# A decoder layer on one core: two self-attention units and one cross-attention unit to a period

## The chip, the core and the metric

The kernel runs on one core of a Trainium2 chip. Its engines work side by side, each through its own queue of instructions: TensorE (PE in the profile, its weight loads PEld) multiplies matrices into the accumulation memory PSUM, VectorE (DVE) and ScalarE (ACT) read PSUM and work element by element, GpSimd (POOL) does element work on SBUF, and SyncE (SP) issues most transfers. Semaphores order the engines among each other. The metric is the time of one execution on the device, in microseconds (us). Three runs of the kernel before took 2284.96, 2285.08 and 2286.03 us; the median is 2285.08.

## The reference

One layer of a decoder for 32 sequences of 256 tokens, width 256, all in float32 but for the feed-forward's quantised products. Cut to what matters:

```python
# self attention: 16 heads of 64, 4 key/value heads, rotary positions, ALiBi, no causal mask
attn = einsum('bhqd,bhkd->bhqk', rope(x @ Wq), rope(x @ Wk)) / sqrt(64) + slopes * (k - q)
x = layernorm(x + merge(softmax(attn) @ v) @ Wo)
# cross attention to ctx: 16 heads of 16, each projection behind its own layer norm,
# windows of 64 (own and preceding), causal, and only between tokens of equal cell number
p = where(mask, rope(qh) @ rope(kh).T / sqrt(16), lowest)
x = layernorm(x + ln(merge(softmax(p) @ vh)) @ w_o.T + b_o)
# feed-forward 256 -> 1024 -> 256: activations rounded to 8 bits, weights to -1, 0, 1
x = layernorm(x + bitlinear(silu(bitlinear(x, w_gate)) * bitlinear(x, w_up), w_down))
```

## The kernel before, in words

A sequence (called a batch, `b`) is worked on in stages, and several batches are under way at a time. Nothing is carried between batches but buffers.

**Self attention.** A batch has eight self units: (128 queries `qc`, key/value pair `kc`, head pair group `rp`), four heads each. `self_scores` multiplies `qT` by `kT` on PE with 64 rows (one head in each half of the array), into two PSUM banks `s`; DVE adds the ALiBi row, negates, and finds the minimum (`p`, `nm`, L410); ACT exponentiates in place and sums (L420). `self_turn` transposes the four heads' `p` on PE (`t`, L447), and ACT copies the result to `pT` (L452). Two units make a pair, and for a pair `self_values` multiplies `v` by `pT` (`o`, L464, 64 columns a head), ACT copies to `oT`; `self_inverse` (DVE) and `self_spread` (PE, `R`, L479) bring the reciprocal sums into shape, and `self_normal` multiplies `oT` by them on DVE. `self_output` multiplies by `Wo` (`wo`, L495), adds the residual, and makes the query of cross attention: stats on DVE, `rs` on POOL (L510 to L513), the normed row `zq` on DVE, its transposition `zqT`, the projection `xq`, `biased` (`qb` on ACT, partition exchange `other` by DMA) and `rotated` (three POOL products).

**Cross attention.** A batch has four cross units (128 queries, half of the heads). `cross_scores` runs 32-row tiles into four banks `xs` (L656); DVE masks and finds the minimum (`xp`, `xnm`, L670); `cross_exp` on ACT (L686), in two halves; `cross_turn` (PE `xt`, L695, ACT `xpT`, L697); `cross_values` with 32-column tiles (`xo`, L711), ACT copies to `xoT`; `cross_back` transposes back (`xr`, L731) and divides on DVE. `cross_output` norms, transposes (`zoT`, ACT copy `zT`), multiplies by the output weights (`xw`, L757) and adds the residual.

**Feed-forward.** `feed_forward` multiplies by gate and up weights in bf16 (`ff`), with tanh on ACT (L812) and products on DVE (L813, L819), quantises through POOL (`tr`, L785; `gu`, L834), transposes by DMA and multiplies by the down weights (`ffo`, L845). `self_inputs` and `cross_inputs` load and project a batch (`proj`, L331; `v`; `zcT`; `xk`; `xv`), two batches' lead ahead.

**The order.** PE, DVE and ACT get their instructions in the order in which the code is run; POOL and SP are ordered by the framework. The order is written by hand in a loop over slots: two slots are a step, a step takes one self unit, and a cross unit begins at every other step. Longer stages are generators; each `yield n` puts the rest n slots later, and they are started at slots counted from `s0 = 16 * b`. `last` holds ACT work that `flush` puts at the end of a slot. All PSUM tiles come from one pool of eight banks. In the even slot of a step:

```python
own(self_turn, step - 1)
if odd:
    cross(cross_back, k - 1)
    cross(cross_turn, k, 0)
else:
    cross(cross_turn, k - 1, 1)
flush()
own(self_scores, step)
if not odd:
    cross(cross_scores, k)
pair(self_values)
```

So, of two steps, one has s, xs and, in its second slot, the projections of other stages and xo; the other has s, o and R.

Of the kernel before, what the change touches and what calls it, by code (L numbers as in the profile page):

```python
# [9 lines left out]
F32 = mybir.dt.float32  # L10
BF16 = mybir.dt.bfloat16
# [5 lines left out]
P = 128  # L17
# [33 lines left out]
def kernel(  # L51
# [33 lines left out]
    def ctile(shape, dtype, name):  # L85
        return const.tile(shape, dtype, name=name, tag=name)
# [6 lines left out]

    ident = ctile([P, P], F32, "ident")
    make_identity(nc, ident)
    ident_b = ctile([P, P], BF16, "ident_b")
    make_identity(nc, ident_b)
    neg_half = ctile([P, 2], F32, "neg_half")
    nc.gpsimd.memset(neg_half, -0.5)

# [285 lines left out]
    def self_scores(b, i):  # L386
        s = state[b]
        qc, kc, rp = self_units[i]
        qT, kT = s["qT", 2 * kc + rp], s["kT"]
        banks = [bank("s") for _ in range(2)]  # L390
        for rr in range(2):
            for half in range(2):
                rows_ = slice(half * HD, (half + 1) * HD)
                nc.tensor.matmul(  # L394
                    banks[half][:, rr * L : (rr + 1) * L],
                    qT[rows_, rr, qc * P : (qc + 1) * P],
                    kT[rows_, kc, :],
                    start=(rr == 0),
                    stop=(rr == 1),
                )  # L400
        s["p", i] = [work("p", [P, 512], 4) for _ in range(2)]
        if rp == 0:
            s["sums", i // 2] = small("sums", 8)
        for half in range(2):
            p = s["p", i][half]
            nm = small("nm", 2)
            for rr in range(2):
                cols = slice(rr * L, (rr + 1) * L)

                nc.vector.tensor_tensor_reduce(  # L410
                    p[:, cols],
                    banks[half][:, cols],
                    alibi[:, 2 * (4 * kc + 2 * rp + rr) + half, :],
                    -0.125,
                    3.0e38,
                    ALU.add,
                    ALU.min,
                    nm[:, rr : rr + 1],
                )
                nc.scalar.activation(  # L420
                    p[:, cols],
                    p[:, cols],
                    AF.Exp,
                    bias=nm[:, rr : rr + 1],
                    scale=-1.0,
                    accum_out=s["sums", i // 2][:, (2 * rp + rr) * 2 + half : (2 * rp + rr) * 2 + half + 1],
                )

    def self_inverse(b, m):

# [58 lines left out]
    def self_output(b, qc):  # L489

        s = state[b]
        py = bank("wo")
        for kc in range(2):
            for r in range(NCH // 2):
                nc.tensor.matmul(  # L495
                    py[:, 0:D],
                    s["oT", qc, kc][:, r, :],
                    wo_sb[:, 4 * kc + r, :],
                    start=(kc == 0 and r == 0),
                    stop=(kc == 1 and r == 3),  # L500
                )
            if kc == 0:
                yield
        h = work("row", [P, D], 6)
        nc.vector.tensor_tensor(h, py[:, 0:D], s["xs"][:, qc, :], ALU.add)
        mv = stats(h, "x1")


        rs = small("rs_x1", 3)
        nc.gpsimd.tensor_scalar(rs[:, 0:1], mv[:, 1:2], EPS, None, ALU.add)  # L510
        nc.gpsimd.tensor_scalar(rs[:, 1:2], mv[:, 1:2], 1.0 + EPS, EPS * EPS, ALU.mult, ALU.add)
        nc.gpsimd.tensor_tensor(rs[:, 0:2], rs[:, 0:2], neg_half, ALU.pow)
        nc.gpsimd.tensor_scalar(rs[:, 2:3], mv[:, 0:1], rs[:, 0:1], -1.0, ALU.mult, ALU.mult)  # L513
        yield
        zq = work("row", [P, D], 6)
        nc.vector.tensor_scalar(zq, h, mv[:, 0:1], rs[:, 1:2], ALU.subtract, ALU.mult)

        s["x1", qc] = x1 = work("x1", [P, D], 4)

        def residual():  # L520
            nc.scalar.activation(x1, h, AF.Identity, bias=rs[:, 2:3], scale=rs[:, 0:1])
            nc.gpsimd.tensor_tensor(x1, x1, xbias[O_], ALU.add)

        last.append(residual)
        yield
        zqT = work("zT", [P, NDC, P])
        transposed(zqT, zq, "zqT")
        yield 2
        pq = bank("xq")
        for ch in range(NDC):  # L530
            for dc in range(NDC):
                nc.tensor.matmul(
                    pq[:, ch * P : (ch + 1) * P],
                    xq_w[:, dc, ch * P : (ch + 1) * P],
                    zqT[:, dc, :],
                    start=(dc == 0),
                    stop=(dc == NDC - 1),
                )
        s["xqT", qc] = work("xqT", [P, NDC, P])
        pair = biased(pq, Q_, P)  # L540
        yield 2
        rotated(s["xqT", qc], *pair, 0, qc * P)


# [25 lines left out]
    def cross_inputs(b):  # L570
# [10 lines left out]
        zc = cs  # L581
        for t in range(NT):
            last.append(partial(scaled, zc[:, t, :], cs[:, t, :], rstds[t]))
        ck = work("ck", [P, L], 1)
        nc.gpsimd.tensor_copy(ck, ck_i)
        yield 2
        zcT = work("tr", [P, NDC, L], 3)
# [156 lines left out]
    def cross_output(b, t):  # L744
        s = state[b]
        on = s["on", t]
        mv = stats(on, "zo")
        rstd = rstd_of(mv, "zo")
        yield
        last.append(partial(scaled, on, on, rstd))  # L750
        yield
        zoT = work("zT", [P, NDC, P])
        transposed(zoT, on, "zoT")
        yield
        py = bank("xw")
        for dc in range(NDC):
            nc.tensor.matmul(py[:, 0:D], zoT[:, dc, :], xo_w[:, dc, :], start=(dc == 0), stop=(dc == NDC - 1))  # L757
        if t == 0:
            s["x2"] = work("x2", [P, NT, D])
        h = s["x2"][:, t, :]  # L760
        nc.vector.tensor_tensor(h, py[:, 0:D], s["x1", t], ALU.add)
        mv = stats(h, "x2")
        rstd = rstd_of(mv, "x2")
        yield
        last.append(partial(scaled, h, h, rstd))


    def feed_forward(b):
# [53 lines left out]
        for t in range(NT):  # L822
# [10 lines left out]
            d_ofs.append(d_of)  # L833
            nc.gpsimd.tensor_scalar(gu[:, t, :], gu[:, t, :], hup, MAGIC, ALU.mult, ALU.add)  # L834
            yield
            hib = work("hib", [P, INNER], 1, BF16)
            nc.vector.tensor_scalar(hib, gu[:, t, :], MAGIC, None, ALU.subtract)
            hiT = work("hiT", [P, NIC, P], 2, BF16)
            nc.sync.dma_start_transpose(hiT, hib)
# [17 lines left out]

    CROSS = 9  # L860
    state = {b: {} for b in range(B)}
    starts = {}

# [7 lines left out]
    for b in range(B):  # L871
        s0 = 16 * b
        if b:
            at(s0 - 16, self_inputs(b))
        at(s0 + 2, cross_inputs(b))
        for t in range(NT):
            at(s0 + 2 * (5 + 4 * t), self_output(b, t))
            at(s0 + 2 * (CROSS + 5 + 4 * t) + 1, cross_output(b, t))
        at(s0 + 2 * (CROSS + 11) + 2, feed_forward(b))

    with tc.manual_schedule(engines={mybir.EngineType.PE, mybir.EngineType.DVE, mybir.EngineType.Activation}):
        running = []
        slot = min(starts)
        while starts or running:
            step, part = divmod(slot, 2)
            k, odd = divmod(step - CROSS, 2)
            for gen in starts.pop(slot, ()):
                running.append([slot, gen])

            def cross(f, unit, *more):  # L890
                if 0 <= unit < 4 * B:
                    f(*divmod(unit, 4), *more)

            def own(f, unit):
                if 0 <= unit < 8 * B:
                    f(*divmod(unit, 8))


            def pair(f):
                if step % 2 == 0 and 0 <= step // 2 - 1 < 4 * B:  # L900
                    f(*divmod(step // 2 - 1, 4))

            if part == 0:
                pair(self_inverse)
            else:
                pair(self_spread)
            if part == 1 and not odd:
                cross(cross_exp, k, 0)
            if part == 0 and odd:
                cross(cross_exp, k, 1)  # L910
            for r in list(running):
                if r[0] == slot:
                    wait = next(r[1], r)
                    if wait is r:
                        running.remove(r)
                    else:
                        r[0] += wait or 1
            if part == 0:
                own(self_turn, step - 1)
                if odd:  # L920
                    cross(cross_back, k - 1)
                    cross(cross_turn, k, 0)
                else:
                    cross(cross_turn, k - 1, 1)
                flush()
                own(self_scores, step)
                if not odd:
                    cross(cross_scores, k)
                pair(self_values)
            else:  # L930
                if not odd:
                    cross(cross_values, k - 1)
                pair(self_normal)
            flush()
            slot += 1

# [88 lines left out]
```

## Time and profile before

The profiled execution took 2288.16 us on the device; its span, from the first to the last instruction, is 2286.3 us. Granted TensorE clock: 0.985 of full over the span.

| engine | busy us | share of the span |
|---|---|---|
| PE | 2186.2 | 96% |
| PEld | 1653.7 | 72% |
| DVE | 1709.6 | 75% |
| ACT | 1692.1 | 74% |
| POOL | 1117.3 | 49% |

A page of the profile shows busy time of each engine, the chain of work that ended last, and groups of equal instructions by line with what ended the idle time before them. The timeline gives instructions in order of time, equal neighbours merged: start, length, engine, line, operation, tiles written and read, and how many. For PE, lengths overlap (a matmul begins before its predecessor's modelled end), so one start is compared with the next. A fp32 product stands there as two instructions. Costliest groups on the engines beside PE: the exponentials (L420) 507.9 us of ACT in 1024 instructions, and the passes over the scores (L410) 372.3 us of DVE in 1024.

### The profile page before, as it was taken

The numbers are of one execution on the slowest core, as the hardware profiler recorded it, in microseconds if no ns is written. First come the engines' busy times: TensorE is split into PE (matmuls) and PEld (weight loads), VectorE is DVE, ScalarE is ACT, GpSimd is POOL, SyncE is SP. The second block draws the span as 40 slices with busy tenths as digits, with TensorE's granted clock in tenths as the row PEclk, the third lists the DMA queues.
The fourth block names the chain that finished last, engine by engine and source line by source line (L and its number), as shares of the span: only waits on it lengthen the run. The fifth ranks groups of instructions, "written<-read, shape, count | busy, mean of one in ns | idle before, by whom it ended". The sixth has DMA issues, their size and how long they took to land.

```text
span 2286.3 us, 55642 instructions
## 1 busy us (share of the span) xinstructions
PE 2186.2 (96%) x17828; PEld 1653.7 (72%) x17828; DVE 1709.6 (75%) x6949; ACT 1692.1 (74%) x4961; POOL 1117.3 (49%) x1851
## 2 busy tenths in 40 slices
PE   7999999999999999999999999999999999999983
PEld 5677777777777777777777777777777777777651
DVE  3767777877777777777777777787777787777675
ACT  2677777878777878777878777778777777777762
POOL 5344555554555444545554545454545454545432
PEclk9999999999999999999999999999999999999986
DMA  6312222222222222222222222222222222222111
GB/s 215 89 52 55 65 67 59 58 58 59 66 66 59 59 58 63 64 64 60 60 58 67 57 64 63 60 57 68 55 65 62 62 54 68 59 57 56 31 31 31
DMA packets 191427, 144.09 MB, mean 63 GB/s; under 512 B 107808, under 2 KB 160928, under 8 KB 191136
## 3 DMA queue, kind: packets, MB, share of 16 engines
q1 hardware_dynamic: 189440, 136.95, 24.3%
q8 instruction: 144, 2.36, 0.4%
q10 hardware_dynamic: 1696, 3.57, 0.4%
q14 instruction: 147, 1.20, 0.2%
HBM read 39.50 MB, written 8.39 MB: 21 GB/s over the span
## 4 chain that ended last, share of the span: by engine, by line
PE 71%; DVE 12%; ACT 11%; DMA 2%; issue 2%; POOL 1%; SPq 0%; ACTq 0%; POOLq 0%; DVEq 0%
PE s L394 10%; PE proj L331 10%; PE wo L495 9%; PE t L447 8%; PE o L464 8%; ACT p L420 4%; DVE p L410 4%; PE xt L695 4%; DVE gu L813 3%; PE xw L757 3%; ACT xp L686 3%; PE xv L616 3%; PE ffo L845 2%; PE R L479 2%; PE xk L604 2%; PE v L363 2%
## 5 line engine op out<-in xcount | busy, mean ns | idle before, releaser
L420 ACT ACTIVATE p<-p,nm 128x256 f32<-128x256 f32 x1024 | 507.9, 498 | 156.1 <-DVE nm L410 152.3
L410 DVE CUSTOM_DVE_ANT_0 p<-s,alibi 128x256 f32<-128x256 f32 x1024 | 372.3, 420 | 167.8 <-PE s L394 167.8
L452 ACT COPY pT<-t 128x512 f32<-128x512 f32 x512 | 274.8, 590 | 190.7 <-PE t L447 190.1
L686 ACT ACTIVATE xp<-xp,xnm 128x128 f32<-128x128 f32 x1024 | 326.0, 394 | 4.3 <-DVE xnm L670 4.3
L394 PE MATMUL s<-kT,qT 64*128 64x256 f32 x2048 | 290.9, 403 | 0.0
L447 PE MATMUL t<-ident,p 128*128 128x128 f32 x2048 | 269.2, 274 | 3.2 <-ACT p L420 3.2
L447 PEld LDWEIGHTS t<-ident,p 128*128 128x128 f32 x2048 | 240.4, 141 | 34.8 <-ACT p L420 6.6
L464 PE MATMUL o<-pT,v 128*64 128x256 f32 x2048 | 249.3, 385 | 0.0
L331 PE MATMUL proj<-xT,wq_sb 128*128 128x256 f32 x1024 | 249.1, 387 | 0.0
L495 PE MATMUL wo<-wo_sb,oT 128*128 128x256 f32 x1024 | 245.3, 382 | 0.0
L355 POOL TENSOR_TENSOR qT<-qT,other 128x512 f32<-128x512 f32 x128 | 163.7, 1279 | 152.0 <-DMA other<-psin 83.7
L670 DVE CUSTOM_DVE_ANT_0 xp<-xs,mask 128x128 f32<-128x128 f32 x1024 | 225.7, 286 | 0.9 <-PE xs L656 0.9
L394 PEld LDWEIGHTS s<-kT,qT 64*128 64x128 f32 x2048 | 176.6, 186 | 54.7 <-issue 32.8
L495 PEld LDWEIGHTS wo<-wo_sb,oT 128*128 128x128 f32 x1024 | 189.4, 190 | 33.8 <-issue 10.6
L331 PEld LDWEIGHTS proj<-xT,wq_sb 128*128 128x128 f32 x1024 | 185.6, 191 | 32.7 <-DVE xnm L670 5.9
L464 PEld LDWEIGHTS o<-pT,v 128*64 128x64 f32 x2048 | 136.0, 136 | 97.4 <-issue 41.1
L420 ACT ACTIVATION_READ_ACCUMULATOR p<-p,nm 128x1 f32 x1024 | 192.4, 188 | 0.0
L340 DVE TENSOR_TENSOR psin<-proj,rs_sb 128x512 f32<-128x512 f32 x160 | 110.2, 689 | 96.7 <-PE proj L331 96.5
L697 ACT COPY xpT<-xt 128x512 f32<-128x512 f32 x256 | 153.6, 600 | 8.3 <-PE xt L695 6.6
L695 PE MATMUL xt<-ident,xp 128*128 128x128 f32 x1024 | 155.1, 275 | 0.0
L566 POOL TENSOR_TENSOR qb<-qb,rx_sb 128x256 f32<-128x256 f32 (+1 forms) x96 | 87.7, 913 | 128.9 <-ACT xp L686 76.6
L813 DVE SCALAR_TENSOR_TENSOR gu<-gu,ff 128x512 f32<-128x512 f32 x128 | 82.1, 681 | 74.6 <-ACT gu L812 74.6
(150 smaller groups left out, 4365.0 us busy)
## 6 DMA issues: line engine op xcount, KB each, us to landing
other<-psin SPq DMA_DIRECT2D x640, 64.0 KB, 2.0
xT<-in_xt_dram SPq DMA_DIRECT2D x32, 256.0 KB, 2.9
xs<-in_x_dram SPq DMA_DIRECT2D x32, 256.0 KB, 3.1
cs<-in_ctx_dram SPq DMA_DIRECT2D x32, 256.0 KB, 2.7
other<-qb SPq DMA_DIRECT2D x64, 128.0 KB, 2.0
kTz<-tr SPq DMA_DIRECT2D x256, 32.0 KB, 2.0
other<-qb SPq DMA_DIRECT2D x128, 64.0 KB, 1.9
out_dram<-x SPq DMA_DIRECT2D x32, 256.0 KB, 2.3
```

What stands on the lines that cost most here:

```text
L331: nc.tensor.matmul(pq[:, c * L : (c + 1) * L], w[:, dc, c * P : (c + 1) * P], xT[:, dc, :], start=(dc == 0), stop=(dc == NDC - 1),)
L355: nc.gpsimd.tensor_tensor(d2, d2, other, ALU.add)
L394: nc.tensor.matmul(banks[half][:, rr * L : (rr + 1) * L], qT[rows_, rr, qc * P : (qc + 1) * P], kT[rows_, kc, :], start=(rr == 0), stop=(r ...
L410: nc.vector.tensor_tensor_reduce(p[:, cols], banks[half][:, cols], alibi[:, 2 * (4 * kc + 2 * rp + rr) + half, :], -0.125, 3.0e38, ALU.add ...
L420: nc.scalar.activation(p[:, cols], p[:, cols], AF.Exp, bias=nm[:, rr : rr + 1], scale=-1.0, accum_out=s["sums", i // 2][:, (2 * rp + rr) * ...
L447: nc.tensor.transpose(pt[:, j * P : (j + 1) * P], p[half][:, rr * L + kk * P : rr * L + (kk + 1) * P], ident,)
L452: nc.scalar.copy(pT[half], pt)
L464: nc.tensor.matmul(po[half * HD : (half + 1) * HD, rp * L : (rp + 1) * L], s["v"][:, kk, (2 * kc + half) * HD : (2 * kc + half + 1) * HD], ...
L495: nc.tensor.matmul(py[:, 0:D], s["oT", qc, kc][:, r, :], wo_sb[:, 4 * kc + r, :], start=(kc == 0 and r == 0), stop=(kc == 1 and r == 3),)
L670: nc.vector.tensor_tensor_reduce(p[:, cols], banks[2 * half + j // 2][:, j % 2 * P : (j % 2 + 1) * P], s["mask"][:, qc, :], -1.0, 3.0e38, ...
L686: nc.scalar.activation(p[:, cols], p[:, cols], AF.Exp, bias=s["xnm", i][half][:, j : j + 1], scale=-1.0)
L695: nc.tensor.transpose(pt[:, j * P : (j + 1) * P], p[:, j * P : (j + 1) * P], ident)
```

## The change

The loop goes over periods of four slots, each with two self units and one cross unit.

- Part 0: the scores of both self units, the values of the preceding pair, its `R`, other stages' parts, `self_normal`, and both halves of the preceding cross unit's transposition. `self_scores` keeps PE and DVE; the exponentials become `self_exp`, called around the values.
- Part 1: other stages' parts, the cross scores, the values of the preceding cross unit, half of the exponentials.
- Part 2: parts, the other half, the first unit's turn, `cross_back`. Part 3: `self_inverse`, parts, the second unit's turn.
- The distance between self and cross attention, `CROSS`, is four periods (16 slots) instead of nine steps (18); output stages start at other slots, and `cross_output` waits two slots ahead of its transposition and of `xw` instead of one each.
- `zq` on DVE moves into the work at the end of its slot. `hib` has two buffers instead of one, the integer cells are turned to float in place instead of in `ck`, and an unused bf16 identity is dropped.

The numbers of units, products, passes and exponentials stay the same. The core of the diff:

```diff
+    def self_exp(b, i, half):
+        s = state[b]
+        p, nm = s["p", i][half], s.pop(("nm", i, half))
+        for rr in range(2):
+            cols = slice(rr * L, (rr + 1) * L)
+            e = (2 * (i % 2) + rr) * 2 + half
+            nc.scalar.activation(
+                p[:, cols],
+                p[:, cols],
+                AF.Exp,
+                bias=nm[:, rr : rr + 1],
+                scale=-1.0,
+                accum_out=s["sums", i // 2][:, e : e + 1],
+            )
...
-        nc.vector.tensor_scalar(zq, h, mv[:, 0:1], rs[:, 1:2], ALU.subtract, ALU.mult)
         s["x1", qc] = x1 = work("x1", [P, D], 4)
         def residual():
+            nc.vector.tensor_scalar(zq, h, mv[:, 0:1], rs[:, 1:2], ALU.subtract, ALU.mult)
...
-        ck = work("ck", [P, L], 1)
+        ck = ck_i.bitcast(F32)
...
         last.append(partial(scaled, on, on, rstd))
-        yield
+        yield 2
         zoT = work("zT", [P, NDC, P])
         transposed(zoT, on, "zoT")
-        yield
+        yield 2
         py = bank("xw")
...
-            hib = work("hib", [P, INNER], 1, BF16)
+            hib = work("hib", [P, INNER], 2, BF16)
...
-    CROSS = 9
+    CROSS = 4
...
-            at(s0 + 2 * (5 + 4 * t), self_output(b, t))
-            at(s0 + 2 * (CROSS + 5 + 4 * t) + 1, cross_output(b, t))
-        at(s0 + 2 * (CROSS + 11) + 2, feed_forward(b))
+            at(s0 + 9 + 8 * t, self_output(b, t))
+            at(s0 + 4 * CROSS + 11 + 8 * t, cross_output(b, t))
+        at(s0 + 4 * CROSS + 26, feed_forward(b))
...
             if part == 0:
+                own(self_scores, 2 * m)
+                own(self_scores, 2 * m + 1)
+                own(self_exp, 2 * m, 0)
+                own(self_exp, 2 * m, 1)
+                own(self_exp, 2 * m + 1, 0)
+                pair(self_values, m - 1)
+                own(self_exp, 2 * m + 1, 1)
+                pair(self_spread, m - 1)
+                parts()
+                pair(self_normal, m - 1)
+                cross(cross_turn, k - 1, 0)
+                cross(cross_turn, k - 1, 1)
+            elif part == 1:
+                parts()
+                cross(cross_scores, k)
+                cross(cross_values, k - 1)
+                cross(cross_exp, k, 0)
+            elif part == 2:
+                parts()
+                cross(cross_exp, k, 1)
+                own(self_turn, 2 * m)
+                cross(cross_back, k - 1)
             else:
+                pair(self_inverse, m)
+                parts()
+                own(self_turn, 2 * m + 1)
             flush()
             slot += 1
```

More of the change, by code (lines that the diff above doesn't have):

```diff
@@ L95 @@
     make_identity(nc, ident)
-    ident_b = ctile([P, P], BF16, "ident_b")
-    make_identity(nc, ident_b)
     neg_half = ctile([P, 2], F32, "neg_half")
@@ L419, in self_scores @@
                 )
[L420 to L427, printed above, removed]
+            s["nm", i, half] = nm
+    def self_exp(b, i, half):
[12 more added lines that the diff above has]
+            )
     def self_inverse(b, m):
@@ L884 @@
         while starts or running:
-            step, part = divmod(slot, 2)
-            k, odd = divmod(step - CROSS, 2)
+            m, part = divmod(slot, 4)
+            k = m - CROSS
             for gen in starts.pop(slot, ()):
@@ L892, in cross, with pair, own @@
                     f(*divmod(unit, 4), *more)
-            def own(f, unit):
+            def pair(f, unit):
+                if 0 <= unit < 4 * B:
+                    f(*divmod(unit, 4))
+            def own(f, unit, *more):
                 if 0 <= unit < 8 * B:
[L896 to L901, printed above, removed]
-            if part == 0:
-                pair(self_inverse)
-            else:
-                pair(self_spread)
@@ L907 @@
[L907 to L933, printed above, removed]
+                    f(*divmod(unit, 8), *more)
@@ new lines, in parts @@
+            def parts():
+                for r in list(running):
+                    if r[0] == slot:
+                        wait = next(r[1], r)
+                        if wait is r:
+                            running.remove(r)
+                        else:
+                            r[0] += wait or 1
+            if part == 0:
+                own(self_scores, 2 * m)
[20 more added lines that the diff above has]
+                cross(cross_back, k - 1)
+            else:
+                pair(self_inverse, m)
+                parts()
+                own(self_turn, 2 * m + 1)
```

## Prediction

> **What bounds the kernel now.** I read the page first: its busy shares, then the chain that ended last.
>
> ```profile
> span 2286.3 us, 55642 instructions
> PE 2186.2 (96%) x17828; PEld 1653.7 (72%) x17828; DVE 1709.6 (75%) x6949; ACT 1692.1 (74%) x4961; POOL 1117.3 (49%) x1851
> PE 71%; DVE 12%; ACT 11%; DMA 2%; issue 2%; POOL 1%; SPq 0%; ACTq 0%; POOLq 0%; DVEq 0%
> ```
>
> PE is busy nearly always and carries 71% of the chain. Busy is no proof that nothing is lost inside it, so next comes PE's timeline in a steady batch, read from one start to the next.
>
> ```profile
> 1008.25 1.89 PE L495 MATMUL wo<-wo_sb,oT 128*128 128x256 f32 x8
> 1009.98 1.04 PE L447 MATMUL t<-ident,p 128*128 128x128 f32 x8
> 1010.85 0.60 PE L695 MATMUL xt<-ident,xp 128*128 128x128 f32 x4
> 1011.38 1.13 PE L394 MATMUL s<-kT,qT 64*128 64x256 f32 x8
> 1012.45 0.69 PE L656 MATMUL xs<-kTz,xqT 32*64 32x256 f32 x16
> 1013.06 1.99 PE L616 MATMUL xv<-xkv_w,tr 128*128 128x256 f32 x8
> 1014.89 1.89 PE L495 MATMUL wo<-wo_sb,oT 128*128 128x256 f32 x8
> 1016.71 0.64 PE L711 MATMUL xo<-xpT,xvaug 128*32 128x128 f32 x16
> 1017.29 1.99 PE L331 MATMUL proj<-xT,wq_sb 128*128 128x256 f32 x8
> ...
> 1020.21 0.60 PE L695 MATMUL xt<-ident,xp 128*128 128x128 f32 x4
> 1020.74 1.13 PE L394 MATMUL s<-kT,qT 64*128 64x256 f32 x8
> 1021.80 1.95 PE L464 MATMUL o<-pT,v 128*64 128x256 f32 x16
> 1023.68 0.66 PE L479 MATMUL R<-ident,wide 128*128 128x128 f32 x4
> ```
>
> Eight full-array 128x256 passes take 1.73 us (1008.25 to 1009.98), 0.216 each; eight transposes take 0.87. Whatever stands beside another tile shape (the numbers such as 64*128) takes more: xt, half of t, takes 0.53 instead of 0.44 ahead of s; s, four pairs of passes, takes 1.07 instead of 0.86; xv behind xs 1.83, wo ahead of xo 1.82, proj behind xo 1.83 instead of 1.73. So **each change of shape costs about 0.19 us**, 0.09 at the end of the old group and 0.10 at the start of the new one.
>
> The steady step from batch to batch is 68.2 us (the same scores, one batch apart in the timeline). Real waits are few. The waits name one pair above all:
>
> ```profile
> PEld xw L757 <- ACT zT L206: 61.6, 63, 3.2
> PE xw L757 <- ACT zT L206: 34.0, 63, 2.9
> ```
>
> The two rows overlap, so I take start distances: in each batch the gate group ahead of one xw takes 1.77 us instead of 0.86, and the projection ahead of the other 2.18 instead of 1.83, together **1.26 us a batch**. Why zT is late stands in the windows and the chain of that stretch:
>
> ```profile
> 1017.30:1034.70 17.40, 16.66 (x155) 11.71 (x152) 13.90 (x55) 15.84 (x47) 6.91 (x12) 1.00 0.24 58
> ```
>
> The columns are length, then PE, PEld, DVE, ACT, POOL busy: ACT works 15.8 of 17.4 us while the feed-forward's tanh shares the stretch with exponentials. Over the batch ACT and DVE are busy 52.7 and 53.3 of 68.2 us.
>
> **What the Trainium skill says.** "TensorEngine Tiling (Array Packing)", Key Properties: a change of the tiling mode, not just of the tile, drains TensorE. The trace agrees, 0.19 us a change. "TensorE: Matmul & The Clock Gate", the table of specifications, gives ScalarE and VectorE strict first-in-first-out queues; the trace agrees: zT's copy, 0.36 us long, is late because exponentials and qb stand before it. "PSUM — Partial Sum Buffer" counts 8 banks in a partition, and the code has eight; where a bank is waited for I follow the built program's semaphores.
>
> **The change, part by part.**
>
> 1. Mode changes. Per pair of units and cross unit, before: xt|s, s|xs, xs|full, full|xo, xo|full, xt|s, s|o, o|R, eight. After: full|s (the two score units adjoin), s|o, o|R; full|xs, xs|xo, xo|full, six. Two fewer are 2 x 0.19 = 0.39 us, and 128 pairs give **-50 us**. The trace shows neither s beside s nor xs beside xo. Bounds: the inner s|s costs 0 to 0.19 and xs|xo 0.1 (the cheap start of xo) to 0.3. I take 0 and the usual change, since s already runs pairs at 0.216 inside and s|o behaves so. The bad end takes back 0.3 a pair, 38 us.
>
> 2. The wait at xw. cross_output now yields 2 ahead of zoT and of xw. In the new PE order t, xr, up, t, both scores, o, R and up stand between zoT and the heavy xw, 9 us of PE. zT is copied in ACT's old order relative to tanh, so it is ready. Gain 1.26 x 31 = **-39 us, were nothing late in its place**.
>
> 3. What is late next. The exponentials stand on ACT around o and are needed by turns two parts later, 8 us on, so that wait is covered by o, R, xt, xs and xo. But both turns' copies now stand at the end of a period, directly ahead of the next scores and o. I add up the period with gate and up (self pairs 3, 7, ... of the numbering) from its first score, 0. PE without waits: scores 1.92, o to 3.80, R 4.30, proj 6.03, zqT 6.25, xt 7.12, gate 7.98, xs 8.71, xo 9.28, xq 10.27, gate 11.13, zoT, t 12.22, xr, up 13.3, t 14.26. DVE: the period before ends with h, the ffs reductions, wide, xvaug, xib, which waits for POOL's tr, and zq, so the first p starts near 2.1 to 2.6 instead of 1.2. Eight p at 0.35 step. ACT (steps in the trace: p 0.49, oT 0.47, xpT and pT 0.48, gu 0.58, xp 0.29, on 0.52, zT and xoT 0.26, qb 0.25) reaches the end of oT and eight p at 7.0 to 7.5, xpT at 8.2 to 8.7, gate's tanh at 9.9 to 10.4; DVE's gu product ends at 10.6 to 11.1, then eight xp at 0.21; ACT exponentiates half of them by 12.2 to 12.7, qb, second tanh 13.8 to 14.3, zT, the other half 15.3 to 15.8, four pT to 17.2 to 17.7. The last t waits for a bank that DVE's second gu product frees at 14.0 to 14.5; the second score unit for banks that pT frees at 15.8 and 16.3 to 16.8; o for the last pT. It starts at 17.2 to 17.7 instead of 16.2: **1.0 to 1.5 us lost**. The next period has 13.8 us of PE and 12.5 of ACT and takes the delay in. In the period with the down projections, qb on ACT waits for xq at 14.6 and holds half of the xp, pT and two scaled rows behind it: o of the next period waits 0.1 to 0.4. Sum 1.1 to 1.9 a batch, middle 1.5: **+47 us**.
>
> 4. Moved or small edits. zq moves behind the parts on DVE, and waits for POOL's rs_x; queued behind it are the eight p of the next period, counted above; in the longer down-projection period the delay (p at 3.9 instead of 1.2) is covered by 16.9 us of PE against 11 of DVE. self_exp apart from self_scores is the same 2048 ACT records. ck over ck_i makes the next ck_i load on SP wait for POOL's mask; behind it on SP are hiT transposes, but the mask is done some 10 us sooner. xqT, kTz and other transfers (2 us to landing on the page) have periods of 14 to 20 us between issue and use; uncovered they would hold xs. hib's second buffer and the unused ident_b: 0. Start-up and tail, some 100 us outside the steady batches, keep their slots: -5 to +5, taken as 0.
>
> Sum: -50 - 39 + 47 = -42. The profiled execution took 2288.2 us (span 2286.3 and 1.9 around it), giving 2246; it lies 3.1 above the median of 2285.1, so on the scale of the median I say **2243**.
>
> **Rivals.** (a) The new waits do not appear, because ACT's copies get done within the bank slack: -50 - 39 = -89, some 2196. For it: ACT is idle a quarter of the batch. Against: in the heavy stretch it has 1.6 us to spare of 17.4. (b) Slower: DVE's p in the gate period start late since zq and xib stand ahead of them and wait for POOL; each us goes through ACT's queue into PE's o. It decides from 0.39 x 4 + 1.26 = 2.8 us of waits a batch on. With p at 4.5 instead of 2.3, waits are 3.7 to 4.1, +1 us a batch, some 2320. For it: POOL's rows show waits on DVE of up to 7.4 us (rs_x) and 5.5 us (tr), so the exchange is slow. Against: my count has DVE at 11 us in a 14.3 us period. (c) No difference: PE waits for banks precisely at the changes of shape, so their removal hides under waits; about 2285. Against: before, no PE wait lies at s, xs or o.
>
> **How the numbers follow.** 0.2% (4.6 us) is about what a measurement of this kernel tells from no change. My forecast, 2225 to 2280: 0.58; (a) and what lies between: 0.22; (b): 0.15; (c): 0.05. Faster 0.80, same 0.05, slower 0.15. The range, from the stall-free 2196 to 2292, leaves out about 0.07 below and 0.13 above.
>
> **What would show it.** Right: s in groups of 16 at 1.92 us ahead of o, xs 0.64 and xo 0.57 adjoining, a steady step of 66.6 to 67.1 us, xw no longer in PE's waits, and in its place o (on pT), t (on DVE gu) or s (on pT) with 1.1 to 1.9 us a batch. Wrong: PE waits over 2.8 us a batch, waits at xs for DMA or POOL, or scores of two units taking over 2.1 us with no wait.

## The result, and the profile after

Four runs of the kernel after took 2303.58 to 2305.49 us, median **2304.53**; four of the kernel before 2284.96 to 2286.03, median 2285.43. The ratio is 1.0083, interval [1.0066, 1.0101]: slower by 0.8%, where 2243 was forecast. The profiled execution of after took 2303.58 us.

The head of the profile page, its busy shares and its shares of the chain:

```profile
span 2301.5 us, 55178 instructions
PE 2190.7 (95%) x17828; PEld 1693.2 (74%) x17828; DVE 1750.0 (76%) x6949; ACT 1670.2 (73%) x4961; POOL 1107.2 (48%) x1849
PE 82%; ACT 6%; DVE 5%; POOL 3%; DMA 2%; issue 2%; SPq 0%; ACTq 0%; POOLq 0%; DVEq 0%
```

PE's share of the chain rose from 71 to 82%, as an order with fewer waits would have it, and still the time is longer. Beside the weight loads, which overlap PE, only DVE's busy time grew by more than a few us: 1709.6 to 1750.0, with the same 6949 instructions. **The same instructions became longer**, three groups of them above all: xib (32 instructions) took 45.1 us instead of 22.9, wide (128) 80.2 instead of 62.4, and zq (64) 37.4 instead of 26.1. What that costs is the rest of this document, in which a single instruction of DVE or POOL is also called a row.

Next the waits of PE from 200 to 2180 us of the kernel after (engine, line, tile waited with, engine and tile waited for: us in total, times, longest):

```profile
PE xs L662 <- ACT zT L204: 17.6, 29, 0.6
PE xs L662 <- ACT oT L477: 8.4, 30, 0.5
PE t L453 <- DVE gu L819: 6.9, 25, 0.3
PE ff L804 <- ACT qb L556: 4.6, 25, 0.2
```

xw is gone. In its place stand four waits for ACT and DVE, about once in a batch each. A batch has four periods, which I call after what other stages put into them: up and the output projection (14.19 us from one block of scores to the next, medians of 24 batches), down (16.82), cross keys and values (20.37), and **gate** (17.43). Without waits PE's work in them is 13.8, 16.9, 20.3 and 14.26 us (the third is counted here in the way in which the prediction counted the others). So three periods lie within 0.4 us of the count, and the gate period is 3.2 over it. PE's timeline of one (start, length, line, tiles, count):

```profile
1019.03 2.00 PE L392 MATMUL s<-kT,qT 64*128 64x256 f32 x16
1020.96 1.95 PE L470 MATMUL o<-pT,v 128*64 128x256 f32 x16
...
1026.15 1.03 PE L804 MATMUL ff<-ff_gate,xiT 128*128 128x512 bf16 x4
1027.46 0.64 PE L662 MATMUL xs<-kTz,xqT 32*64 32x256 f32 x2 [0.28 <-ACT oT L477]
1028.70 1.15 PE L662 MATMUL xs<-kTz,xqT 32*64 32x256 f32 x14 [0.61 <-ACT zT L204]
1029.79 0.65 PE L717 MATMUL xo<-xpT,xvaug 128*32 128x64 f32 x32
...
1035.44 1.09 PE L453 MATMUL t<-ident,p 128*128 128x128 f32 x8 [0.28 <-DVE gu L819]
1036.46 2.35 PE L392 MATMUL s<-kT,qT 64*128 64x256 f32 x16
```

The bracketed idle times are small, but the starts say more: from xs to xo 2.33 us pass, where 16 of these passes take 0.64 elsewhere, and gate ahead of xs takes 1.31 instead of 0.86. xs waits for banks that ACT's copies oT and zT free; by xo some 2 of the 3.2 us are lost, and the rest is lost by the end of the period, at up and at the last t. ACT's timeline shows why they are late:

```profile
1023.87 0.51 ACT L426 ACTIVATE p<-p,nm 128x256 f32<-128x256 f32 x1 [3.54 <-DVE nm L408]
...
1026.84 0.56 ACT L477 COPY oT<-o 128x512 f32<-128x512 f32 x1
...
1028.30 0.35 ACT L204 COPY zT<-zqT 128x256 f32<-128x256 f32 x1
```

ACT stood idle for 3.54 us until DVE's first pass over the scores was done, 4.84 us after the scores began; oT is queued behind six exponentials. And DVE and POOL ahead of that pass:

```profile
1018.77 1.07 DVE L441 COPY wide<-rinv 128x512 f32<-128x512 f32 x1
1019.76 0.74 DVE L630 TENSOR_TENSOR xvaug<-xv,xbias 128x256 f32<-128x256 f32 x2
1020.67 1.49 DVE L793 TENSOR_SCALAR xib<-tr 128x512 bf16<-128x512 f32 x1 [0.17 <-POOL tr L791]
1022.08 0.41 DVE L176 BATCH_NORM_STATS2 st<-on 128x6 f32<-128x256 f32 x1
...
1022.63 0.81 DVE L526 TENSOR_SCALAR row<-row,mv_x,rs_x 128x256 f32<-128x256 f32 x1
1023.36 0.41 DVE L408 CUSTOM_DVE_ANT_0 p<-s,alibi 128x256 f32<-128x256 f32 x1
```

```profile
1018.29 1.27 POOL L353 TENSOR_TENSOR qT<-qT,other 128x512 f32<-128x512 f32 x1
1019.53 1.10 POOL L791 TENSOR_SCALAR tr<-x,ffup 128x256 f32<-128x256 f32 x2
1020.61 1.27 POOL L572 TENSOR_TENSOR qb<-qb,rx_sb 128x512 f32<-128x512 f32 x1
1021.84 1.45 POOL L573 TENSOR_TENSOR other<-other,rx_sb 128x512 f32<-128x512 f32 x1
```

DVE has almost no idle time here: one wait of 0.17 us for POOL's tr. It works through wide (1.07 us), xib (1.49) and zq (named row, 0.81), each while a product of POOL is running. wide begins inside POOL's qT, xib 0.06 us after POOL's qb, and zq inside POOL's other; each ends within 0.3 us of that product's end. The passes (p) take 0.41 us here as everywhere. They start at 1023.36, **4.3 us after the scores**.

### The profile page after: what moved, and what is told of

The parts are those of the page before. It is cut to its first block, busy times and chain, and to the rows that moved or that the text cites. A ratio compares the mean times of both kernels' runs of the same rounds, so it can differ in the third digit from the quotient of the medians.

```text
span 2301.5 us, 55178 instructions
## 1 busy us (share of the span) xinstructions
PE 2190.7 (95%) x17828; PEld 1693.2 (74%) x17828; DVE 1750.0 (76%) x6949; ACT 1670.2 (73%) x4961; POOL 1107.2 (48%) x1849
## 3 DMA queue, kind: packets, MB, share of 16 engines
q8 instruction: 142, 2.33, 0.4%
## 4 chain that ended last, share of the span: by engine, by line
PE 82%; ACT 6%; DVE 5%; POOL 3%; DMA 2%; issue 2%; SPq 0%; ACTq 0%; POOLq 0%; DVEq 0%
PE proj L329 11%; PE s L392 10%; PE wo L501 10%; PE o L470 9%; PE t L453 9%; PE xt L701 4%; PE xs L662 4%; PE ff L804 3%; ACT p L426 3%; PE xo L717 3%; PE R L485 3%; PE xq L538 3%; PE ffo L851 3%; PE xk L610 2%; PE xw L763 2%; PE v L361 2%
## 5 line engine op out<-in xcount | busy, mean ns | idle before, releaser
L408 DVE CUSTOM_DVE_ANT_0 p<-s,alibi 128x256 f32<-128x256 f32 x1024 | 362.0, 417 | 29.6 <-PE s L392 29.6
L458 ACT COPY pT<-t 128x512 f32<-128x512 f32 x512 | 267.2, 594 | 69.3 <-PE t L453 69.1
L392 PE MATMUL s<-kT,qT 64*128 64x256 f32 x2048 | 264.5, 390 | 0.0
L453 PEld LDWEIGHTS t<-ident,p 128*128 128x128 f32 x2048 | 233.7, 141 | 33.1 <-DVE gu L819 20.0
L392 PEld LDWEIGHTS s<-kT,qT 64*128 64x128 f32 x2048 | 197.1, 186 | 37.6 <-issue 17.1
L470 PEld LDWEIGHTS o<-pT,v 128*64 128x64 f32 x2048 | 146.9, 136 | 91.4 <-issue 21.5
L426 ACT ACTIVATION_READ_ACCUMULATOR p<-p,nm 128x1 f32 x1024 | 199.0, 194 | 0.0
L662 PE MATMUL xs<-kTz,xqT 32*64 32x256 f32 (+1 forms) x1536 | 126.1, 412 | 30.2 <-ACT zT L204 17.6
L726 ACT COPY xoT<-xo 128x256 f32<-128x256 f32 x128 | 47.5, 371 | 140.9 <-PE xo L717 140.8
L703 ACT COPY xpT<-xt 128x512 f32<-128x512 f32 x256 | 136.9, 588 | 9.6 <-PE xt L701 5.8
```

The source lines that it names most:

```text
L392: nc.tensor.matmul(banks[half][:, rr * L : (rr + 1) * L], qT[rows_, rr, qc * P : (qc + 1) * P], kT[rows_, kc, :], start=(rr == 0), stop=(r ...
L408: nc.vector.tensor_tensor_reduce(p[:, cols], banks[half][:, cols], alibi[:, 2 * (4 * kc + 2 * rp + rr) + half, :], -0.125, 3.0e38, ALU.add ...
L426: nc.scalar.activation(p[:, cols], p[:, cols], AF.Exp, bias=nm[:, rr : rr + 1], scale=-1.0, accum_out=s["sums", i // 2][:, e : e + 1],)
L453: nc.tensor.transpose(pt[:, j * P : (j + 1) * P], p[half][:, rr * L + kk * P : rr * L + (kk + 1) * P], ident,)
L458: nc.scalar.copy(pT[half], pt)
L470: nc.tensor.matmul(po[half * HD : (half + 1) * HD, rp * L : (rp + 1) * L], s["v"][:, kk, (2 * kc + half) * HD : (2 * kc + half + 1) * HD], ...
```

## Experiments

The theory under test: the gate period's loss is carried by the start of DVE's passes, and that start is late because xib, zq and wide, lengthened beside POOL's products, stand ahead of them. The rivals: the passes are late since DVE waits for POOL's results (the mechanism of the prediction's rival b); or the passes don't matter, and the loss comes from ACT's queue, the banks or the later steps of `cross_output`. All kernels start from after, but for the one named. Ratios are to the kernel before on the same chip.

### What stands ahead of the passes

**zq behind the passes.** `behind` is a list of works run after both `self_scores` of part 0; the short form of the edit:

```diff
         def residual():
-            nc.vector.tensor_scalar(zq, h, mv[:, 0:1], rs[:, 1:2], ALU.subtract, ALU.mult)
...
+        behind.append(partial(nc.vector.tensor_scalar, zq, h, mv[:, 0:1], rs[:, 1:2], ALU.subtract, ALU.mult))
```

> The changed kernel, with DVE's zq row put behind the eight score passes of the next period instead of ahead of them. Names: the gate period is the one with the gate products (17.43 us from scores to scores in the changed kernel, 14.26 of PE work). Theory 1 (DVE's queue: xib, stats and zq stand ahead of the score passes, which start 4.3 us into the gate period, and each us goes through ACT into PE): the passes start 0.8 us sooner, the gate period takes 16.6 us, the step from batch to batch 68.0 instead of 68.8, the whole about 2279 us. Theory 2 (ACT's own load in the gate period is the bound, wherever it starts): gate period 17.3 or more, about 2302 us. Theory 3 (DVE is lengthened by POOL beside it): no difference to theory 1 here, but zq's length falls from 0.81 to 0.41 us where POOL is idle.

2299.42 us, ratio 1.0057 [1.0042, 1.0072]. In the gate period the passes start at +3.59 and it takes 16.68, both 0.7 less. But in the down period zqT now waits for zq (16.82 to 17.41): zq moved for both query halves, and only one needed it.

**xib between the two units' passes**, with its DMA transposes:

```diff
-        nc.vector.tensor_scalar(xib, xi, MAGIC, None, ALU.subtract)
+        between.append(rounded)   # rounded() issues xib and its transposes
...
                 own(self_scores, 2 * m)
+                run(between)
                 own(self_scores, 2 * m + 1)
```

> The changed kernel, with DVE's xib (and its two transposing DMAs) put between the score passes of the two units of the next period. Theory 1: the first four passes start 1.5 us sooner; the other four stay where they are, so half of the exponentials come sooner and ACT idles some 0.5 us between; gate period 16.2 us, step 67.6, about 2267 us. Theory 2: gate period 17.3 or more, about 2302 us. A loss is possible if xiT lands after its first gate product: 2.3 us from issue to landing, against 2.5 us left; then a PE wait on that DMA of up to 1 us appears at the gate product.

2288.22 us, ratio 1.0008 [1.0000, 1.0017]. The passes start at +2.91, the gate period takes 16.83: 0.6 gained of 1.4, as the gate products now wait for xib's transposes:

```profile
PE ff L813 <- DMA xiT<-xib: 26.5, 28, 2.0
```

**Both.**

> The changed kernel with both moves: xib between the two units' score passes, zq behind them. Theory 1: passes start near 2.0 us into the gate period, gate period 15.4 us, step 66.8, about 2243 us. Theory 2: gate period 17 or more, about 2295 to 2302 us.

2262.76 us, ratio 0.9897 [0.9882, 0.9911]: passes at +1.93, gate period 15.43. Together they bring more than the sum of each alone, as with zq out of the way xib is issued 1 us sooner, and its transposes are in time. The down period keeps the wait for zq (17.41).

**Both, but zq behind the passes for the first query half alone** (`if qc == 0`, the half of the gate period).

> The changed kernel with xib between the two units' score passes, and zq behind them only for the first 128 queries (whose zq falls into the gate period); for the other half zq stays ahead of them, since behind them it came too late for zqT (0.6 us a batch of PE waiting at zqT with both behind). Theory 1: period with the down projections back at 16.8 us, gate period 15.4, step 66.8, about 2244 us, 1.8% faster than before. If zqT's wait was not due to zq's place: 2263 us.

2246.21 us, ratio 0.9823 [0.9808, 0.9837]. Periods 14.19, 16.82, 20.37, 15.43: the down period is whole again, nothing else moved. Moving the start of the passes, while ACT's work and the steps of `cross_output` stayed as they were, took away 2.0 of the gate period's 3.2 us; for these the second rival is out as the cause. ACT's queue and the banks are the way on which the delay reaches PE.

**xib on ACT**, at the end of its slot, nothing else moved:

```diff
-        nc.vector.tensor_scalar(xib, xi, MAGIC, None, ALU.subtract)
+            nc.scalar.activation(xib, xi, AF.Identity, bias=neg_magic, scale=1.0)
```

> The changed kernel with one operation on another engine: xib, DVE's 1.41 us row ahead of the score passes, becomes an ACT row behind the second unit's pT copies and x1, where ACT idles 3.5 us. Theory 1 (what stands on DVE ahead of the passes sets PE's loss, near 1 us for 1 us): passes start 2.7 to 2.9 us into the gate period instead of 4.3, gate period 15.9, step 67.3, about 2258 us. Theory 2 (ACT's load is the bound): ACT has 0.6 us more to do in this stretch, gate period 17.4 or more, 2304 us or more.

2263.70 us, ratio 0.9900 [0.9885, 0.9914]. Passes at +2.91, gate period 16.03. ACT does xib in 0.72 us, where DVE took 1.49. So ACT had more to do than in after, and the gate period still became 1.4 us shorter: ACT's load was not what bound it. The waits that are left are for gu, which comes behind the passes on DVE.

**xib on ACT and zq behind for the first half.**

> The kernel after with two edits of earlier runs together: zq behind the passes for the first query half alone, and xib computed on ACT at the end of its slot, so that neither stands ahead of the passes. The order of PE stays. If the gate period's loss is carried by the start of the passes, they start at +1.2 to +1.4 us (from +1.95 with zq moved alone and +2.91 with xib on ACT alone), and at 0.9 us of PE for each us the gate period falls from 15.43 to about 14.8, the step to 66.2, the time to 2246 - 0.6 x 32 = 2227. If the remaining loss of 15.43 against 14.26 counted is already set by ACT's queue (the waits of t for the product gu), 0.7 us more work on ACT in that period makes it 15.4 to 16.0 and the time 2246 to 2264.

**2234.66 us, ratio 0.9772 [0.9756, 0.9788]**, the fastest kernel of this study, and faster than both given ones. The gate period is 15.08, between the two expectations. The passes did not start at 1.2 to 1.4 but at +1.96, as with xib between them: I had forgotten that the statistics of `on` (0.56 us) and a wide of 1.07 still stand ahead. So what fell (15.43 to 15.08) can't come from that start; the last pass ends at +4.79 instead of +5.72, as xib no longer stands between the two units.

Here are the kernels in which the passes of both units follow one another directly and PE's order is that of after (the third is told of below):

| kernel | passes start | gate period | difference |
|---|---|---|---|
| after | 4.32 | 17.43 | 13.11 |
| zq behind | 3.59 | 16.68 | 13.09 |
| no rotation | 3.34 | 16.45 | 13.11 |
| xib on ACT | 2.91 | 16.03 | 13.12 |
| xib on ACT, zq behind for one half | 1.96 | 15.08 | 13.12 |

**From the first pass to the next scores the chain takes 13.1 us, whatever stands ahead of it**; in the range measured, each us of delay is a us of PE. By this PE's own 14.26 us would bind only with a start before 14.26 - 13.11 = 1.15, which no run with this order of PE reached.

### Is it POOL that lengthens the rows?

The cross keys' rotation, POOL's three products qb, other and tr, left out (the unrotated keys go on, so that this part of the computation is missing); DVE's instructions stay:

```diff
-        kT = work("tr", [P, NDC, L], 3)
-        rotated(kT, *pair, 1, 0)
+        kT = pair[0].rearrange("p (c t) -> p c t", t=L)
```

> The changed kernel without the rotation of the cross keys on POOL (three products of 1.27 us each a batch, that run beside wide, xib and zq); the keys go to kTz unrotated, so this part of the computation is left out. Theory 3 (DVE's copy and scalar operations from SBUF to SBUF wait for a port that POOL holds): xib falls from 1.41 to about 0.75 us, zq from 0.58 to 0.45 in the mean, the score passes start 1.2 us sooner, gate period 16.2 us, step 67.6, about 2267 us. If xib is long for another reason: it stays at 1.3 or more and the whole within 5 us of 2304.

2273.97 us, ratio 0.9947 [0.9932, 0.9962]; passes at +3.34, gate period 16.45. The groups by shape, of DVE, of after and then of this kernel (count | busy us, mean ns | idle before, releaser):

```profile
L793 DVE TENSOR_SCALAR xib<-tr 128x512 bf16<-128x512 f32 x32 | 45.1, 1411 | 5.4 <-POOL tr L791 5.3
L526 DVE TENSOR_SCALAR row<-row,mv_x,rs_x 128x256 f32<-128x256 f32 x64 | 37.4, 584 | 1.5 <-POOL rs_x L518 1.5
```

```profile
L792 DVE TENSOR_SCALAR xib<-tr 128x512 bf16<-128x512 f32 x32 | 28.1, 879 | 5.4 <-POOL tr L790 5.4
```

xib falls from 1411 to 879 ns, with the same wait for tr of 5.4 us in 32, 0.17 in each: the passes came 1 us sooner without a change in what DVE waits for. zq fell to 386 ns; wide, which stands beside the rotation of self attention (kept), stayed at 626. xib's remaining length was made by another product that moved up beside it, POOL's residual. In one batch xib came first, and then it is POOL that was held (DVE, then POOL):

```profile
1078.92 0.43 DVE L792 TENSOR_SCALAR xib<-tr 128x512 bf16<-128x512 f32 x1 [0.17 <-POOL tr L790]
1079.82 0.38 DVE L526 TENSOR_SCALAR row<-row,mv_x,rs_x 128x256 f32<-128x256 f32 x1
```

```profile
1078.94 0.99 POOL L528 TENSOR_TENSOR x<-x,xbias 128x256 f32<-128x256 f32 x1
```

xib takes 0.43 us when it starts 0.02 us ahead of the product, and the product 0.99 instead of the 0.72 of the other batches. So the one that starts later is held for most of the other's time. In the kernel before, the start of xib inside a product (POOL, then DVE, of two batches) drifts, and its length with it:

```profile
947.88 1.27 POOL L568 TENSOR_TENSOR tr<-qb,other 128x512 f32<-128x512 f32 x1
948.05 1.39 DVE L787 TENSOR_SCALAR xib<-tr 128x512 bf16<-128x512 f32 x1
```

```profile
537.76 1.28 POOL L568 TENSOR_TENSOR tr<-qb,other 128x512 f32<-128x512 f32 x1
538.65 0.67 DVE L787 TENSOR_SCALAR xib<-tr 128x512 bf16<-128x512 f32 x1
```

In both, xib ends 0.3 us (0.29 and 0.28) behind the product's end, as it does in after; in the three last batches, with no product beside it, it takes 0.42 to 0.43. So its length is **what is left of the product, and 0.3 us**, which is a little less than it takes alone. The Trainium skill says this under "SBUF — State Buffer", Who interferes with whom: VectorE's second pair of ports is GpSimd's only one, it is locked for a whole instruction, and copy, cast and tensor_scalar can take modes that need it. The runs agree: a copy (wide) and tensor_scalar (xib, zq) became longer, the passes over scores in PSUM did not (0.41 to 0.42 us in after). The lock itself no run shows, only its effect on the times.

POOL has a part in the delay beside this. In after, tr ends 1.60 us after the scores and xib starts at 1.64, while xvaug, the row ahead of it, ends at 1.47 even behind the long wide. With a short wide DVE would only have waited longer for tr, so wide's 0.64 us cost nothing there; it is xib and zq whose lengthening moved the passes.

### The two promised gains

**xo beside xs in the kernel before**, one change of shape less in each pair, nothing else:

```diff
                 if not odd:
                     cross(cross_scores, k)
+                    cross(cross_values, k - 1)
                 pair(self_values)
             else:
-                if not odd:
-                    cross(cross_values, k - 1)
                 pair(self_normal)
```

> The kernel before, with the cross values of the preceding unit called straight behind the cross scores: one change of shape fewer in each of 128 pairs, and nothing else of the change. The price of a change (0.19 us) says: step from batch to batch 67.5 instead of 68.2 us, the whole about 2261 us (-24); xs to xo 0.64, xo 0.57. If a removed change only lets PE wait elsewhere (xo on xpT, whose copy has 2 us left): step 68.2, the whole 2285 or more.

2292.11 us, ratio 1.0025 [1.0017, 1.0033]: slower. Two of a batch's four pairs became 0.20 us shorter (14.24 to 14.04, 19.82 to 19.62), which is the price of a change of shape to 0.01; the other two became 0.26 and 0.27 longer, and PE's wait at xw grew from 29.6 to 53.3 us (200 to 2180 us):

```profile
PE xw L757 <- ACT zT L206: 53.3, 58, 3.2
```

The change of shape is real PE time, but in the two pairs around xw it comes back as waiting for ACT's zT. That is what the prediction's rival (c) says of the removed changes, that they hide under waits, though the wait is for a copy and not for a bank.

**The old `yield` in `cross_output`**, both places, in the kernel after.

> The changed kernel with cross_output's old waits of one slot ahead of its transposition and of xw. The prediction's step 2 (the two-slot yields alone take the wait at xw away): it comes back, 1.26 us a batch, about 2343 us, PE waiting for zT at xw. The other reading (in the new order the place of zT's copy on ACT decides, and PE is late anyhow in the gate period): within 10 us of 2304, little or no wait at xw.

2383.76 us; the ratio, of three of its four runs, is 1.0383 [1.0316, 1.0450]. The four took 2355 to 2391 us with granted clocks of 0.942 to 0.964, where after has 0.982 to 0.984, so only the direction and the wait are used. The wait stands at zoT, not at xw as I had thought, and is larger than the one of before:

```profile
PE zoT L203 <- ACT on L197: 92.8, 56, 3.2
```

That is 3.3 us a batch (92.8 / 28 batches), where the same view of the kernel before has 1.0 at xw (29.6 / 29): in the new order the longer yields are needed. Both were put back together; which of the two is needed is not shown.

### Three orders that fell short

**The output stage of self attention first in every slot** (the running stages are sorted), on the kernel with zq behind for one half and xib between, so that zq's inputs are ready sooner and the tail shorter.

> The last kernel, with self_output's part run ahead of the other stages' parts in every slot, so that DVE's row and POOL's rs_x no longer stand behind the feed-forward's reductions and its 1024-element product. For the steady batches: step 66.4 to 66.8. For the tail: the changed kernel's end, from its last score block on, takes 117.7 us against 109.0 before, with PE idle 5.3 us at zqT for rs_x; if that order is the cause, it falls to about 113, the whole to about 2235 us; if not, it stays at 117 and the whole at 2244 or more.

2316.03 us, ratio 1.0133 [1.0116, 1.0150]. Passes at +1.17, the best of all, but periods of 17.91 (down) and 16.25 (gate), and the tail unchanged. Sorting moved zqT ahead of proj on PE as well, 1.7 us sooner, and now PE waits for zq:

```profile
PE zqT L209 <- DVE row L195: 34.1, 29, 1.6
PE zqT L209 <- DVE row L533: 23.5, 29, 0.8
```

**The same, with the stages sorted in one slot of 16, two slots ahead of the gate period**, and **that with xib on ACT.** The transposition was meant to stay behind the projection. But the sort reorders the list of running stages for good, so `self_output` stayed ahead of the projection in the gate period's own slot too, and these two kernels don't test what they were made for.

> The kernel with xib between the score passes and the first half's zq behind them, with self_output run first in the one slot (of 16) of the row that precedes the gate period: DVE's row and stats and POOL's rs_x and tr come sooner, and the transposition stays behind the projection on PE (when self_output was first everywhere, zqT stood ahead of the projection and waited 1.2 us for zq). Theory 1: the passes start at 1.2 to 1.4 us into the gate period instead of 1.95, gate period 14.7 to 15.0, step 66.2, about 2228 us. If the loss that is left (15.4 against 14.3 of PE work) is ACT's: 15.4, 2246 us.

> The last kernel with xib on ACT ahead of the exponentials instead of on DVE between the passes. Theory 1: the second unit's passes come 0.4 to 1.0 us sooner; gate period 14.5 to 14.8, step 66.0, about 2222 us. If ACT is what is left of the bound, the 0.6 us of xib on ACT lengthen the gate period by up to that: 15.2, about 2240 us.

2295.37 us, ratio 1.0037 [1.0025, 1.0049], and 2267.42, ratio 0.9914 [0.9901, 0.9927]; both missed by 45 to 67 us. The gate period is 17.56 (the median; it swings between 15.5 and 19.2) and 16.09 although the passes start at +1.28 in both. Waits of the first, and of the second:

```profile
PE zqT L209 <- DVE row L195: 52.2, 29, 2.6
```

```profile
PE zqT L211 <- DVE row L197: 28.4, 28, 1.2
```

I had kept in mind the start of the passes and missed what the sort does to PE's order: zqT follows R at once, and zq, behind eight passes and beside the rotation (1.23 us in the median of the first kernel, 1.31 of the second), is not there. The same zq is on time in the kernels where proj stands ahead of zqT.

## Why the prediction was wrong

- **Step 1, changes of shape: right.** Scores of two units take 1.93 us (1019.03 to 1020.96; 1.92 counted) and o follows, xs and xo adjoin at 0.64 and 0.58 where nothing waits. Three periods agree with the count within 0.4 us, and the run on the kernel before gave 0.20 us for one change fewer in each of the two pairs that PE bounds.
- **Step 2, the wait at xw: right** that it goes with the longer yields; without them it comes back at zoT.
- **Step 3, what is late next: the step that failed, in one term.** It said that "the first p starts near 2.1 to 2.6 instead of 1.2". It starts at 4.32. The sum behind that term held: from p at 2.1 to 2.6 and o at 17.2 to 17.7 the working has 15.1 us, and o begins 1.92 after the scores, so 13.2 from the first pass to the next scores; 13.1 was measured in five kernels. With 4.3 in its place the same sum gives 17.5 for the gate period; it took 17.43. o, the end point of the working, began at 19.7 (1038.75 less 1019.03), where the sum gives 19.4. The place of the loss was not foreseen: the working has xs at 8.71 without a wait and expects waits at t, s and o. But it also has oT and eight p done 4.9 us after the first pass; from 4.32 on that is 9.2, later than xs, and xs is where PE waited first.
- **What was mis-sized:** the rows ahead of the passes. xib starts at 1.64, when tr is there, and this wait the working names. It prints no lengths of the rows; beside those of before, xib took 1.49 us instead of 0.67 (the median), and zq 0.81 instead of 0.41. Between the two stand the statistics of `on`, 0.55, which the working doesn't name. Together these are 1.8 us, and 4.32 less 1.8 is 2.5, inside the stated 2.1 to 2.6. wide was 0.64 longer too, but that was covered by the wait for tr. Before already had the sign: the shapes' spread for xib there (min/median/max ns).

```profile
L787 DVE TENSOR_SCALAR xib<-tr x32: 417/666/1386, 197.5 to 2257.3; 128x512 bf16<-128x512 f32 x32
```

```profile
L793 DVE TENSOR_SCALAR xib<-tr x32: 426/1485/1491, 194.5 to 2272.3; 128x512 bf16<-128x512 f32 x32
```

The first line is of the kernel before, the second of the one after: the same instruction ranges from 0.42 to 1.39 us in the one and from 0.43 to 1.49 in the other. In before it mostly began 0.9 us into a product of the rotation, so that the rest of it, 0.4 us, was all that counted; the new order starts it 0.06 us into one in nearly every batch.

- **Sum.** Step 3 allowed 1.5 us of waits a batch. The step is 68.81 us against the 66.9 that the working has (68.2 - 1.56 - 1.26 + 1.5), 1.9 more; over some 28 steady batches that is 53 of the 61 us between 2243 and 2304.5. Start and tail below are 2.6 more, and some 5 come from the working's having taken its gains of about 1.3 us a batch for 31 to 32 batches and not for 28.
- **Rival (b) had the outcome and the place** (the passes of the gate period start late, past 2.8 us of waits a batch the kernel loses), and a start of 4.5 for the 4.3 measured. The 4.5 was supposed and not worked out, so that its nearness is luck. The mechanism, more waiting for POOL's results than step 3 has, was not it: DVE's wait for tr is 0.17 us, and tr is there at 1.60, which fits step 3's own start; what came on top is the length of the rows. I held it at 0.15 because "my count has DVE at 11 us in a 14.3 us period". That argued from a share: the 13.1 us chain begins with DVE's first pass, so DVE's place in time mattered and not how full it was.
- **Start and tail, taken as 0: not quite.** The first four batches are 6.2 us shorter (from the first scores to the 16th pair's after it, 244.55 against 250.75), and the end, from the scores of the last pair, 8.8 longer (117.7 against 108.9). Part of that is 5.3 us in which PE waits at zqT for a zq whose input stands on DVE behind the feed-forward's reductions. Sorting the stages did not shorten the tail (118.4); the rest of its cause is open.

## What to carry to other kernels

Before moving an instruction of VectorE, look at what GpSimd does at its new place: read the shortest and longest of its durations and not the mean, and if the longest is beside a GpSimd product, count what is left of the product wherever the instruction starts inside one. But ask too whether the next row would have waited anyway, as xib did behind wide. When an order of work is repeated, look for the first instruction of the chain that ends in its next round; a us ahead of that instruction costs a us, while the same us behind it may be free. And when a row is moved out of the way, its consumer on another engine has to stay where the row can reach it.

## What the runs showed of the hardware

- A tensor_scalar of 128x512 takes 0.43 us on VectorE alone and 1.49 with a GpSimd product started 0.06 us earlier; started 0.02 us ahead of one, it takes 0.43 and the product is lengthened instead, 0.72 to 0.99. In these runs the order of start decides who pays.
- Started 0.06, 0.17 and 0.89 us into a GpSimd product of 1.27 us, it took 1.49, 1.39 and 0.67 us: what was left of the product, and 0.3 us.
- ScalarE does the same rounding in 0.72 us, also when it starts 0.06 us into the same GpSimd product.
